# Splitting a burst of attention scores: the third PSUM bank is computed three places later, behind another item's values' product

## The chip, the cores and the metric

The kernel runs on one core of a Trainium2 chip. The metric is the device time of one execution in microseconds. TensorE (PE) multiplies matrices into PSUM, VectorE (DVE), ScalarE (ACT) and GpSimd (POOL) work elementwise, SyncE (SP) issues most transfers. In the profile "PE" is the matmuls and "PEld" the loads of weights that go before them.

## The reference, cut to what matters

x has 4 batches of 4096 rows of 512. Three stages follow one another, each added to x: half a feed-forward, a local attention with 16 heads of 32, and half the same feed-forward again.

```python
x = x + 0.5 * ffn(layernorm(x))          # 512x512, inputs and weights quantised in blocks of 32 (fp6 grid)
x = x + attn(layernorm(x))
x = x + 0.5 * ffn(layernorm(x))

# attn: row i sees the 13 rows nbr[i] around it in its batch
qkv  = x @ qkv_w.T + qkv_b               # q scaled by 32 ** -0.5
attn = einsum('bhld,bhlkd->bhlk', q, k[:, :, nbr]) + rpb[:, bidx]
out  = einsum('bhlk,bhlkd->bhld', softmax(attn), v[:, :, nbr])
out  = out @ proj_w.T + proj_b
```

## The kernel before, in words

**Products.** Every full product (`product`, line 151) splits both operands into a high and a low half-precision part and sums three of the four combinations: 12 matmuls of 128x128 by 128x512 into one PSUM bank. They share a pool of three banks (tag `mm`). Per tile of 128 rows there are two feed-forward products (`pmf`), one for values (`pmv`) and one for the attention's output (`pmo`); per item of attention there are two more, for queries and keys (`pmqk`).

**Items.** Attention is cut into items: four tiles of rows (a group of 512) by four heads, 128 items `m` in all, and an item comes along as often as a tile does. Within a group, queries are taken in blocks of 30, each with a window of 42 keys: 16, 17 or 18 blocks per group (`group_blocks`).

**Scores.** For each block, `softmax(m)` issues eight matmuls at line 437, two for each of four heads: weights are 32x32 (the queries), the moving side is 84 or 42 columns. The result `ps` has a pool of one buffer of three PSUM banks; six blocks lie in each bank. VectorE then adds the bias table (line 462) and the second part (line 465) into `sf`. The row maximum (469), its subtraction on GpSimd (471), Exp on ScalarE (473), the sum and its reciprocal on VectorE (476 to 478), the scaling on GpSimd (480), two casts on ScalarE (484, 485), a subtraction on GpSimd (487) and a transposing DMA (489) make the weights `pT`. `attend(m)` multiplies them with the stacked values at line 507: four matmuls per block, 126 rows by 32 columns of weights, 30 columns moving, into `pv`; ScalarE (534) and VectorE (540) put the result into `ring`, from which `pmo` reads.

**Order.** The main part keeps the order in which the program issues. That order is laid out by hand in slots: `begin(slot, stage, rank)` puts a stage in a slot, `run_slot` runs the stages of a slot in order of rank, and `yield n, rank` sends the rest of a stage n slots on. A tile, and an item with it, takes `STEP` = 7 slots. With k = 7m an item's queries and keys start at slot k + 38, its scores at k + 42 (rank 6) and its values' product at k + 59 (rank 6). So in one turn of seven slots TensorE runs: feed-forward, scores of item m, `pmo`, `pmqk`, the values' product of item m - 2, `pmqk`, feed-forward, `pmv`, and again. Each engine works through its own queue in this order and waits where an input is missing.

Of the kernel before, what the change touches and what calls it, by code (L numbers as in the profile page):

```python
# [32 lines left out]
ALU = mybir.AluOpType  # L33
# [9 lines left out]
KN = QN + NK - 1  # L43
QR = 32
KV = 3 * KN
GROUP = 4
GT = GROUP * P
MAXB = 18
PSB = 6
# [15 lines left out]
def macaron_kernel(  # L65
# [12 lines left out]
    nc = tc.nc  # L78
# [4 lines left out]
    D = dim // HEADS  # L83
# [42 lines left out]
    table = const.tile([P, 3, KC, KN], F32, name="table")  # L126
    halo = const.tile([P, KC, 2, 2, KN], F16, name="halo")

    def bc(t, n):

        return t.unsqueeze(2).to_broadcast([t.shape[0], t.shape[1], n])
# [191 lines left out]
    def span(j):  # L323

        q0 = min(j * QN, length - QN)
        return q0, min(max(q0 - NS, 0), length - KN)

    def kind(j):
        return 1 if j == 0 else 2 if j == n_blocks - 1 else 0

    def late(j):

        return QR - QN if j == n_blocks - 1 else 0
# [3 lines left out]
    for g in range(NG):  # L337
        first = done
# [6 lines left out]
    n_items = n_batch * NG * KC  # L345
    qk, probs, stacks = {}, {}, {}

    def item_of(m):

        g, c = divmod(m, KC)  # L350
        return g // NG, g % NG, c
# [69 lines left out]
    def softmax(m):  # L421

        b, g, c = item_of(m)
        j0, j1 = group_blocks[g]
        n = j1 - j0
        t = qk.pop(m)


        ps = ps_s.tile([P, 3, 2, 256], F32, tag="s", name=f"ps{m}")
        for i in range(n):  # L430
            q0, k0 = (KN + at - g * GT for at in span(j0 + i))
            q0 -= late(j0 + i)
            u, w = divmod(i, PSB)
            for part, sides in ((0, 2), (1, 1)):
                for h in range(4):
                    rows = slice(h * D, (h + 1) * D)
                    nc.tensor.matmul(  # L437
                        ps[rows, u, :sides, w * KN : (w + 1) * KN],
                        t[rows, 0, part, q0 : q0 + QR], t[rows, 1, :sides, k0 : k0 + KN],
                        start=part == 0, stop=part == 1,  # L440
                    )

        def pieces(i, e):

            while i < e:
                u, w = divmod(i, PSB)
                whole = max((e - i) // PSB, 1) if w == 0 else 1
                f = min(e, (u + whole) * PSB)
                yield slice(u, u + whole), slice(w, w + (f - i) // whole)
                i = f  # L450

        yield 1, 9
        sf = sfp.tile([P, MAXB, KN], F32, tag="sf", name=f"sf{m}")
        s4 = sf.rearrange("p (u w) k -> p u w k", w=PSB)
        p4 = ps[:, :, :, : PSB * KN].rearrange("p u a (w k) -> p a u w k", k=KN)
        first = 1 if kind(j0) == 1 else 0
        last = n - (1 if kind(j1 - 1) == 2 else 0)
        for i, e in ((0, first), (first, last), (last, n)):
            for u, w in pieces(i, e):
                o = s4[:, u, w, :]  # L460
                bias = table[:, kind(j0 + i), c, :].unsqueeze(1).unsqueeze(1).to_broadcast(o.shape)
                nc.vector.tensor_tensor(o, p4[:, 0, u, w, :], bias, ALU.add)
        for u, w in pieces(0, n):
            o = s4[:, u, w, :]
            nc.vector.tensor_tensor(o, o, p4[:, 1, u, w, :], ALU.add)
        yield 1, 2
        s = sf[:, :n, :]
        top = sm.tile([P, MAXB], F32, tag="top", name=f"top{m}")
        nc.vector.tensor_reduce(top[:, :n], s, AX.X, ALU.max)
        yield 1, 4  # L470
        nc.gpsimd.tensor_tensor(s, s, bc(top[:, :n], KN), ALU.subtract)
        yield 1, 9
        nc.scalar.activation(s, s, AF.Exp, scale=alpha)
        yield 1, 4
        total = sm.tile([P, MAXB], F32, tag="total", name=f"total{m}")
        nc.vector.tensor_reduce(total[:, :n], s, AX.X, ALU.add)
        nc.vector.reciprocal(total[:, :n], total[:, :n])
        nc.vector.tensor_tensor(total[:, :n], total[:, :n], p_scale[:, :n], ALU.mult)  # L478
        yield 1, 4
        nc.gpsimd.tensor_tensor(s, s, bc(total[:, :n], KN), ALU.mult)  # L480
        yield 2, 8
        p = p_tile
        ph = p[:, :n, :KN]
        nc.scalar.copy(ph, s)
        nc.scalar.copy(p[:, :n, 2 * KN : KV], ph)
        yield 2, 4
        nc.gpsimd.tensor_tensor(p[:, :n, KN : 2 * KN], s, ph, ALU.subtract)  # L487
        pT = ptp.tile([P, MAXB, P], F16, tag="pT", name=f"pT{m}")
        nc.sync.dma_start_transpose(out=pT[:, :n, :], in_=p[:, :n, :].rearrange("p n k -> p (n k)"))
        probs[m] = pT  # L490
# [89 lines left out]
    def out_slot(t):  # L580


        i = t - LAST
        if i >= 0:
            return (n_items - 1) * STEP + PV + 3 + 2 * i
        if i >= 1 - GROUP:
            return LAST * STEP + PV + 21 + 4 * i
        return t * STEP + OUT
# [10 lines left out]
    for t in range(NT):  # L599
# [8 lines left out]
        at = out_slot(t)  # L608
# [8 lines left out]
    for m in range(n_items):  # L617
        k = m * STEP
        begin(k + QK, project_qk(m))
        begin(k + SC, softmax(m), 6)  # L620
        begin(k + PV, attend(m), 6)
    for n in range(n_batch * NG):
        k = n * GROUP * STEP
        b, g = divmod(n, NG)
# [4 lines left out]
    with tc.tile_pool(name="setup", bufs=1) as sp, tc.tile_pool(name="scratch", bufs=2) as scr:  # L629
# [12 lines left out]
        rows = {}  # L642

        sq = sp.tile([P, 5 * KC], F32, name="sq")
        first = min(slots)
# [5 lines left out]
        for o in chunks:  # L651
            w, i = (qkv_w, o) if o < 3 * KC else (proj_w, o - 3 * KC)
# [87 lines left out]
        def large(name, o, dt=F32):  # L740
            return scr.tile(
                [P, NB, QB], dt, tag=name, bufs=3 if name == "wu_" else KC, name=f"{name}{o}"
            )

        for o in range(KC):
# [5 lines left out]
            qh, q0 = large("wqh_", o, F16), large("wq0_", o)  # L751
            nc.vector.tensor_tensor(qh, fwb, per(w_r), ALU.mult)
            for i, b in enumerate((w_hi, w_lo)):
                u = large("wu_", f"{o}_{i}")
# [164 lines left out]
```

## Time and profile before

| | us |
|---|---|
| three runs | 2378.66, 2388.48, 2392.82 |
| median | 2388.48 |
| profiled execution, its own time | 2398.3 |
| span of the profiled execution | 2396.5 |
| mean granted TensorE clock in it | 0.990 |

The span runs from the first to the last instruction that the profiler saw; the execution's own time is 1.8 us longer. One turn of seven slots takes about 17.7 us (the scores at 1206.31 and at 1224.00), and 128 turns make up nearly all of the span. In the timeline, a group's duration contains the modelled end of its last matmul and overlaps the next group; differences of starts are the safer reading. A few records of matmuls are missing, so a burst of 144 may be listed with fewer. A wait "<-issue" is idle time for which the profile shows no event that ended it.

### The profile page before, as it was taken

To read this page: it belongs to the slowest core of one execution; us is meant where nothing else is said; L and a number is where in the kernel's file an instruction comes from. 1 tells how busy PE (TensorE), PEld (TensorE's weight loads), DVE (VectorE), ACT (ScalarE), POOL (GpSimd) and SP (SyncE) were. 2 spreads that over 40 slices of the span, in tenths; PEclk is the share of its full clock that TensorE was granted. 3 is DMA by queue.
4 is the path that set the end of the run, shared out by engine and by line. 5 is a ranking of instruction groups with operands and counts; after the bars stand their busy time and mean duration, and the time that the engine had idled before them with its cause. 6 is when DMAs were issued, how large, how long until landed. Compare 5 with 4: busy or idle time off the path is not lost.

```text
span 2396.5 us, 82360 instructions
## 1 busy us (share of the span) xinstructions
PE 2285.3 (95%) x35539; PEld 1118.5 (47%) x35539; DVE 2020.8 (84%) x3588; ACT 1329.8 (55%) x2080; POOL 1990.2 (83%) x2012
## 2 busy tenths in 40 slices
PE   0799999999999999999999999999999999999998
PEld 0344444444444444444444444444444444444443
DVE  8789888888888888888888888888888878888886
ACT  4466555555555555555555555555555555555542
POOL 5578888888888888888888888888888888888886
PEclk9899999999999999999999999999999999999999
DMA  5789788777777777777777778877777786777773
GB/s 153 143 151 155 159 164 159 159 148 151 150 155 158 158 142 150 148 155 156 164 147 149 148 159 161 156 159 146 150 151 158 158 158 131 149 150 152 137 116 108
DMA packets 925701, 360.59 MB, mean 150 GB/s; under 512 B 718876, under 2 KB 889752, under 8 KB 925336
## 3 DMA queue, kind: packets, MB, share of 16 engines
q1 hardware_dynamic: 924992, 354.79, 74.3%
q8 instruction: 278, 4.55, 0.8%
q10 hardware_dynamic: 344, 0.53, 0.1%
q14 instruction: 87, 0.71, 0.1%
HBM read 110.15 MB, written 67.29 MB: 74 GB/s over the span
## 4 chain that ended last, share of the span: by engine, by line
PE 92%; DVE 4%; issue 1%; DMA 1%; POOL 1%; ACT 1%; SPq 0%; DVEq 0%; POOLq 0%; ACTq 0%
PE pmqk L151 28%; PE pmf L151 26%; PE pmo L151 14%; PE pmv L151 14%; PE ps L437 7%; PE pv L507 3%; DVE fw L756 0%; DMA x<-hln 0%; DVE hlq L204 0%; DVE stn L180 0%; DVE whl L786 0%; DMA fw<-in_L_ffn_weight_dram 0%; DVE sc L239 0%; POOL yq L251 0%; DVE x L279 0%
## 5 line engine op out<-in xcount | busy, mean ns | idle before, releaser
L151 PE MATMUL pmf<-wt,xT 128*128 128x512 f16 x3048 | 703.2, 381 | 12.9 <-DMA xT<-hlq 10.3
L151 PE MATMUL pmqk<-x,wt 128*128 128x512 f16 x3072 | 709.3, 381 | 4.8 <-DMA x<-hln 4.6
L151 PEld LDWEIGHTS <-xT 128*128 128x128 f16 x3048 | 298.8, 98 | 377.1 <-DMA xT<-hlq 12.7
L151 PEld LDWEIGHTS <-wt 128*128 128x128 f16 x3072 | 290.6, 98 | 342.7 <-issue 10.4
L151 PE MATMUL pmo<-wt,ring 128*128 128x512 f16 x1536 | 360.5, 385 | 8.5 <-issue 8.5
L151 PE MATMUL pmv<-wt,x 128*128 128x512 f16 x1536 | 354.1, 380 | 4.9 <-DVE mvn L181 4.9
L246 POOL TENSOR_TENSOR yq<-yq,r 128x1024 f32<-128x1024 f32 (+1 forms) x141 | 246.7, 1750 | 131.1 <-DVE r L244 131.1
L568 POOL TENSOR_TENSOR x<-x,half_ffn_b 128x512 f32<-128x512 f32 x256 | 327.8, 1280 | 0.1
L279 DVE SCALAR_TENSOR_TENSOR x<-pmf,coef,x 128x512 f32<-128x512 f32 x256 | 179.7, 702 | 151.9 <-PE pmf L151 151.6
L534 ACT ACTIVATE ring<-pv 128x510 f16<-128x510 f32 (+8 forms) x224 | 82.6, 415 | 396.6 <-PE pv L507 396.6
L314 ACT CAST vt<-pmv 128x512 f16<-128x512 f32 x128 | 75.1, 587 | 389.2 <-PE pmv L151 389.2
L180 DVE BATCH_NORM_STATS2 stn<-x 128x6 f32<-128x512 f32 x384 | 265.4, 691 | 9.0 <-DMA x<-in_L_attn_x_dram 0.2
L251 POOL TENSOR_TENSOR yq<-q,sc 128x1024 f32<-128x1024 fp8e4 (+1 forms) x141 | 246.9, 1751 | 1.0 <-ACT q L249 1.0
L151 PEld LDWEIGHTS <-x 128*128 128x128 f16 x1536 | 150.7, 98 | 187.6 <-DMA x<-hln 5.4
L377 DVE SCALAR_TENSOR_TENSOR qk<-pmqk,qk_b,qk 128x512 f16<-128x512 f32 x256 | 190.7, 745 | 52.9 <-ACT qk L373 51.8
L151 PEld LDWEIGHTS <-ring 128*128 128x128 f16 x1536 | 141.6, 99 | 173.2 <-issue 19.9
L480 POOL TENSOR_TENSOR sf<-sf,total 128x714 f32<-128x714 f32 (+2 forms) x128 | 178.8, 1397 | 42.8 <-DVE total L478 22.9
L186 POOL TENSOR_SCALAR rsq<-mv 128x2 f32<-128x2 f32 (+1 forms) x141 | 130.0, 922 | 99.3 <-DVE mv L181 96.9
L249 ACT ACTIVATE q<-yq,nudge 128x1024 fp8e4<-128x1024 f32 (+1 forms) x141 | 150.3, 1066 | 112.0 <-POOL yq L246 103.8
L373 ACT ACTIVATE qk<-pmqk,qk_b 128x512 f16<-128x512 f32 x256 | 176.5, 689 | 52.2 <-PE pmqk L151 50.4
L233 ACT ACTIVATE yq<-x,nbq,rsq 128x512 f32<-128x512 f32 x254 | 193.6, 806 | 18.3 <-POOL nbq L192 17.6
L487 POOL TENSOR_TENSOR p<-sf,p 128x714 f16<-128x714 f32 (+2 forms) x128 | 192.8, 1506 | 0.1
(145 smaller groups left out, 3466.3 us busy)
## 6 DMA issues: line engine op xcount, KB each, us to landing
vs<-vd SPq DMA_DIRECT2D x144, 357.0 KB
x<-in_L_attn_x_dram SPq DMA_DIRECT2D x128, 256.0 KB
vd<-vt SPq DMA_DIRECT2D x128, 256.0 KB
out_dram<-x SPq DMA_DIRECT2D x128, 256.0 KB
vs<-vd SPq DMA_DIRECT2D x24, 378.0 KB
vs<-vd SPq DMA_DIRECT2D x24, 315.0 KB
rows<-in_L_attn_qkv_w_dram SPq DMA_DIRECT2D x12, 256.0 KB
xT<-hlq SPq DMA_TRANSPOSE x141
```

Source lines behind the costliest of these rows:

```text
L151: nc.tensor.matmul(pm, lhs(a, c), rhs(b, c), start=(n == 0), stop=(n == 3 * KC - 1))
L180: nc.vector.bn_stats(st, xs[t])
L233: nc.scalar.activation(y[:, u], xs[t], AF.Identity, bias=nb[:, u : u + 1], scale=rs[:, u : u + 1])
L246: nc.gpsimd.tensor_tensor(yb, yb, bc(r, QB), ALU.mult)
L251: nc.gpsimd.tensor_tensor(yb, q8.rearrange("p u (n q) -> p (u n) q", q=QB), bc(sc, QB), ALU.mult)
L279: nc.vector.scalar_tensor_tensor(xs[t], pm, cf, xs[t], ALU.mult, ALU.add)
L373: nc.scalar.activation(t[:, s, 0, KN:], pms[s], AF.Identity, bias=bias)
L377: nc.vector.scalar_tensor_tensor(t[:, s, 1, KN:], pms[s], bias, t[:, s, 0, KN:], ALU.add, ALU.subtract)
L437: nc.tensor.matmul(ps[rows, u, :sides, w * KN : (w + 1) * KN], t[rows, 0, part, q0 : q0 + QR], t[rows, 1, :sides, k0 : k0 + KN], start=par ...
L480: nc.gpsimd.tensor_tensor(s, s, bc(total[:, :n], KN), ALU.mult)
L487: nc.gpsimd.tensor_tensor(p[:, :n, KN : 2 * KN], s, ph, ALU.subtract)
L568: nc.gpsimd.tensor_tensor(xs[t], xs[t], b, ALU.add)
```

## The change

The scores of an item's first two banks (`cut` = 12 blocks) and their additions stay where they were. The scores of the third bank (4 to 6 blocks, so 32 to 48 matmuls) are issued three slots after the first two banks with rank 7, which is right behind the values' product of item m - 2; their additions come a slot later. The row maximum and all that follows up to the scaling are three slots later than before, the casts and what follows them two (one of two spare slots is dropped). The last two items keep the old form. No matmul is added or removed.

```diff
         ps = ps_s.tile([P, 3, 2, 256], F32, tag="s", name=f"ps{m}")
-        for i in range(n):
+        def scores(i0, e0):
+            for i in range(i0, min(e0, n)):
...
-        yield 1, 9
         sf = sfp.tile([P, MAXB, KN], F32, tag="sf", name=f"sf{m}")
...
-        for i, e in ((0, first), (first, last), (last, n)):
-            for u, w in pieces(i, e):
+        def add(i0, e0):
+            for i, e in ((0, first), (first, last), (last, n)):
+                for u, w in pieces(max(i, i0), min(e, e0)):
+                    o = s4[:, u, w, :]
+                    bias = table[:, kind(j0 + i), c, :].unsqueeze(1).unsqueeze(1)
+                    nc.vector.tensor_tensor(
+                        o, p4[:, 0, u, w, :], bias.to_broadcast(o.shape), ALU.add
+                    )
+            for u, w in pieces(i0, min(e0, n)):
                 o = s4[:, u, w, :]
...
-        for u, w in pieces(0, n):
-            o = s4[:, u, w, :]
-            nc.vector.tensor_tensor(o, o, p4[:, 1, u, w, :], ALU.add)
+                nc.vector.tensor_tensor(o, o, p4[:, 1, u, w, :], ALU.add)
+        cut = 2 * PSB if m < n_items - 2 else MAXB
+        scores(0, cut)
+        yield 1, 9
+        add(0, cut)
+        if cut < n:
+            yield 2, 7
+            scores(cut, n)
+            yield 1, 9
+            add(cut, n)
         yield 1, 2
...
         nc.gpsimd.tensor_tensor(s, s, bc(total[:, :n], KN), ALU.mult)
-        yield 2, 8
+        yield 1 if cut < n else 2, 8
         p = p_tile
```

In the built program, VectorE has 46 instructions more (3631 for 3585); the other engines have as many as before.

More of the change, by code (lines that the diff above doesn't have):

```diff
@@ L429, in softmax @@
         ps = ps_s.tile([P, 3, 2, 256], F32, tag="s", name=f"ps{m}")
-        for i in range(n):
[L431 to L441, printed above, removed]
+        def scores(i0, e0):
+            for i in range(i0, min(e0, n)):
+                q0, k0 = (KN + at - g * GT for at in span(j0 + i))
+                q0 -= late(j0 + i)
+                u, w = divmod(i, PSB)
+                for part, sides in ((0, 2), (1, 1)):
+                    for h in range(4):
+                        rows = slice(h * D, (h + 1) * D)
+                        nc.tensor.matmul(
+                            ps[rows, u, :sides, w * KN : (w + 1) * KN],
+                            t[rows, 0, part, q0 : q0 + QR], t[rows, 1, :sides, k0 : k0 + KN],
+                            start=part == 0, stop=part == 1,
+                        )
         def pieces(i, e):
@@ L457, in softmax @@
         last = n - (1 if kind(j1 - 1) == 2 else 0)
-        for i, e in ((0, first), (first, last), (last, n)):
-            for u, w in pieces(i, e):
-                o = s4[:, u, w, :]
-                bias = table[:, kind(j0 + i), c, :].unsqueeze(1).unsqueeze(1).to_broadcast(o.shape)
-                nc.vector.tensor_tensor(o, p4[:, 0, u, w, :], bias, ALU.add)
-        for u, w in pieces(0, n):
-            o = s4[:, u, w, :]
-            nc.vector.tensor_tensor(o, o, p4[:, 1, u, w, :], ALU.add)
+        def add(i0, e0):
[5 more added lines that the diff above has]
+                        o, p4[:, 0, u, w, :], bias.to_broadcast(o.shape), ALU.add
+                    )
+            for u, w in pieces(i0, min(e0, n)):
+                o = s4[:, u, w, :]
+                nc.vector.tensor_tensor(o, o, p4[:, 1, u, w, :], ALU.add)
[8 more added lines that the diff above has]
+            add(cut, n)
         yield 1, 2
```

## The prediction

> **What bounds the kernel now.** I read the page's engine table first, then the chain that ended last.
>
> ```profile
> PE 2285.3 (95%) x35539; PEld 1118.5 (47%) x35539; DVE 2020.8 (84%) x3588; ACT 1329.8 (55%) x2080; POOL 1990.2 (83%) x2012
> PE 92%; DVE 4%; issue 1%; DMA 1%; POOL 1%; ACT 1%; SPq 0%; DVEq 0%; POOLq 0%; ACTq 0%
> q8 instruction: 278, 4.55, 0.8%
> ```
>
> TensorE is 95% busy and carries 92% of the chain. So the time is the sum of what TensorE issues, plus its gaps; the other engines matter only if they make it wait. The third line comes back below. Next I took the timeline of TensorE alone around one item (start, us, and how many matmuls).
>
> ```profile
> 1203.63 2.75 PE L151 MATMUL pmf<-wt,xT 128*128 128x512 f16 x12
> 1206.31 1.35 PE L437 MATMUL ps<-qk 32*32 32x84 f16 x144
> 1207.59 2.76 PE L151 MATMUL pmo<-wt,ring 128*128 128x512 f16 x12
> 1210.19 2.75 PE L151 MATMUL pmqk<-x,wt 128*128 128x512 f16 x12
> 1212.88 0.72 PE L507 MATMUL pv<-pT,vs 126*32 126x30 f16 x72
> 1213.54 2.76 PE L151 MATMUL pmqk<-x,wt 128*128 128x512 f16 x12
> ...
> 1224.00 1.22 PE L437 MATMUL ps<-qk 32*32 32x84 f16 x128
> 1225.15 2.76 PE L151 MATMUL pmo<-wt,ring 128*128 128x512 f16 x12
> ```
>
> Differences of starts are what counts. A product of 12 matmuls takes 2.59 us before another product, 2.68 to 2.69 before a small burst (1206.31 - 1203.63; 1212.88 - 1210.19): 0.09 more. The scores take 1.28 us for 144 matmuls and 1.15 for 128, so 8.2 ns each (8.25 in the ns records) and 0.09 that does not depend on the number. The values' product takes 0.66 for 72 and, around 462.60, 0.62 for 68: 8.3 ns each and 0.06 fixed. A product after a burst loses 0.01 more. So each way into or out of a small burst costs 0.06 to 0.10 us in which nothing is issued.
>
> Last, TensorE's waits (engine and line, waited for: us in total, times, longest), one such wait in the timeline, and the granted clock in three stretches (the number before the last two; in front of it busy time of PE, PEld, DVE, ACT, POOL).
>
> ```profile
> PE ps L437 <- issue: 9.3, 7, 3.4
> PE pmo L151 <- issue: 8.5, 4, 4.7
> PE pv L507 <- issue: 1.2, 1, 1.2
> PE pmqk L151 <- issue: 0.2, 1, 0.2
> ```
>
> ```profile
> 826.85 1.32 PE L437 MATMUL ps<-qk 32*32 32x84 f16 x139
> 831.58 0.23 PE L437 MATMUL ps<-qk 32*32 32x84 f16 x5 [3.41 <-issue]
> ```
>
> ```profile
> 820.00:850.00 30.00, 26.59 (x341) 12.32 (x342) 20.68 (x37) 14.00 (x23) 21.64 (x23) 0.94 0.69 137
> 1020.00:1050.00 30.00, 27.95 (x447) 13.41 (x446) 21.47 (x40) 15.28 (x25) 22.76 (x23) 0.94 0.84 170
> 1960.00:1990.00 30.00, 25.35 (x311) 11.51 (x310) 19.64 (x35) 11.91 (x20) 19.53 (x18) 0.89 0.71 134
> ```
>
> TensorE stops 13 times for nothing that a semaphore explains, 19.2 us in all, mostly late in a scores burst or just after one. I read these as waits for instructions. Queue 8 carries 278 packets of 16.4 KB (4.55 MB / 278); TensorE has 2 x 35539 = 71078 matmuls and loads, 256 per packet, 64 bytes each. Counted along the trace, the long waits lie whole multiples of 256 instructions apart within a few (2814, or 10.99 packets, from 739.82 to 831.58). At 831.58 work resumes 1.3 us after a packet that landed at 830.26. Packets start never closer than 3.4 us to each other and take 0.9 to 1.9, so a packet's worth of instructions that is used up faster than about 4 us can run dry. A product uses 24 instructions in 2.6 us and cannot; a scores burst has 256 to 288 instructions in 1.1 to 1.3 us and can. After the three longest waits the clock falls (0.94, 0.94, 0.89 over 30 us): the products behind them run some 6 us longer (10 matmuls of pmo at 1030.15 take 3.81 us where 2.16 is usual). Waits and slow products: about 25 us of the profiled execution.
>
> **The change part by part.** *TensorE.* No matmul is added. The items (126 of 128; the last two keep the old form) have 16, 17 or 18 blocks: 16, 80 and 32 items in all. Before: products, scores 128 to 144, pmo, pmqk, values' product 64 to 72, pmqk. After: scores 96, pmo, pmqk, values' product, scores 32 to 48, pmqk. The ways in and out are 0.09 + 0.09 + 0.01 for the scores and 0.09 + 0.06 + 0.01 for the values' product before: 0.35 us. After, the first is the same; the second is 0.09 + x + 0.09 + 0.01, with x the passage from the values' product straight to scores. The change costs x + 0.03 an item. No row shows x. From below: 0, if one small burst follows another with no gap: 0.03 x 126 = 3.9 us. From above: the dearest edge, scores to product, 0.10: 16.4 us. I take 0.06, since what ends there is the values' product, whose own edge is 0.06 in this trace: 0.092 x 126 = 11.6 us lost. A gain from x is excluded, because a passage cannot take less than nothing.
>
> The Trainium skill, "TensorEngine Tiling (Array Packing)", Key Properties, says that changing the tiling mode drains TensorE. The rows agree that edges cost 0.06 to 0.10 us; by the rule the new edge, 126 x 32 tiles to 32 x 32 tiles, is a drain too, x is not 0, and the sum is 11.6 to 16.4, not 3.9.
>
> *Instruction waits.* The longest dense stretch shrinks from 256 to 288 instructions to 192, and the values' product with the third bank behind it is 192 (16 blocks), 216 (17) or 240 (18). I laid the 256-instruction boundaries over both orders and added the durations above. Before, 23 packets are used up in under 3 us, ten of them in 1.05 us, and 39 in under 5. After, one in under 3 (2.8), 8 in under 5. Of the 12 long waits, nine follow packets used up in under 2.3 us; three (3.5 us of waits together) follow packets of 3.6 to 6.2 us, of which the changed order has about as many. So some 3.5 us stay and about 22 go, in the profiled execution.
>
> The Trainium skill, "Runtime: NRT & Kernel Launch", Instruction fetch mechanics, says that crossing a 16 KiB boundary is mostly hidden. By it the 19.2 us of issue waits are no fetches, nothing is gained, and the time is 2400; the spacing of 256 and the landing at 830.26 are why I go by the rows.
>
> *VectorE.* The two additions are cut at the same bank for 16 and 17 blocks; for 18 blocks there are two more instructions, 46 in the kernel. From 756 elements at 0.94 us to 504 at 0.67 and 252 at 0.37, each cut adds 0.1: 5 us over the kernel, beside TensorE. Cover: VectorE is at 15.5 of 17.7 us per item. The third bank's addition waits for TensorE, and behind it stand put_low of Q, the ring's low part and the row maximum. put_low frees one of three PSUM buffers; at 1215.04 + 0.75 it is done 2.9 us before the product that reuses it (1218.72), and I find it at most 0.8 later. Without the cover each us late is 126 us.
>
> *The chain behind the scores* (maximum, subtraction, Exp, sum, scaling) moves three places later on VectorE, GpSimd and ScalarE, and the casts, the subtraction and the transposing DMA two. GpSimd has 2.3 us free per item, spent before the layer norm's factors, which wait for TensorE. With two subtractions (1.58 and 1.46) now behind the factors and the scaling ahead of them, the multiplication at line 246 starts some 0.6 us later (its wait of 0.94 goes), and the feed-forward input it leads to has some 5 us in hand. The transpose of pT was issued at 1211.21, took 2.86, and is used at 1230.43: of 16 us in hand about 5 go. On SP it passes only the stores and loads of two places; the next store behind it is some 5 us off. All this I cost at nothing.
>
> *The third bank's wait.* In the built order its first matmul waits for VectorE, with the second pmqk queued behind. If that is the first two banks' addition, it was done at 1209.80 before (longer then) and is wanted at 1213.54: 3.7 us of cover, cost nothing.
>
> **The sum.** Profiled execution: 2398.3 - 22 + 11.6 = 2388. The median of the runs, 2388.48, is 9.8 lower than the profiled execution. The steady products agree to a few ns, so I put this to fewer instruction waits: 25 - 9.8 = 15 in a median run, of which some 2 stay and 13.5 go. 2388.5 - 13.5 + 11.6 = 2386.6; I say 2386, 0.1% faster. The spread of the three runs, 14 us, should shrink.
>
> **The rivals.** *Waits stay.* Place: the new 192 to 240 instruction burst and the other packets of 3 to 6 us. Decides if a packet takes over about 5 us from need to use, as the 1.2 us waits behind packets of 4.9 and 6.2 us hint; against it, most such packets pass without wait. Price: no gain, 2388.5 + 11.6 = 2400, and with x = 0.10, 2405. Slower; 0.19 with the small chance that a VectorE wait (0.1 us an item is 13 us) eats its cover. *The passage is free and the waits go.* x near 0, the median as full of waits as the profile: 2388.5 - 22 + 3.9 = 2370; with only 15 there, 2379. Faster, for which both sizes must fall well; 0.17. *Both cancel*, the forecast: 2377 to 2400; 0.64.
>
> The range takes in x from 0 to 0.10 and waits from all gone to nearly all kept: 2372 to 2401. A run of this kernel can tell about 0.5% (12 us) from no change; faster 0.17, within 0.64, slower 0.19.
>
> **What would show it.** Right: issue waits of TensorE fall from 19 to about 4 us and the clock's dips in mid-span vanish; scores to pmo take 0.88 us for 96; from the start of the values' product to the second pmqk it is 1.05 us for 68 and 40 matmuls (68 x 8.3 ns + 0.06 + 40 x 8.25 ns + 0.09), and 0.99 if x is 0. Wrong: semaphore waits of TensorE in mid-span, or issue waits at the third bank.

## The result, and the profile after

The changed kernel takes 2402.4 us (median of 7 runs, 2398.3 to 2404.6), the kernel before 2390.1 us in its 7 runs: the ratio is 1.0056, with a 95% interval from 1.0035 to 1.0078. It is slower by 12 to 13 us, where 4 less than the 2390 was forecast and 2401 was the upper end.

The page after: the engines, and the chain that ended last.

```profile
PE 2291.2 (96%) x35539; PEld 1123.8 (47%) x35539; DVE 2065.4 (86%) x3634; ACT 1324.5 (55%) x2080; POOL 1985.5 (83%) x2012
PE 86%; DMA 6%; DVE 4%; POOL 2%; ACT 1%; issue 1%; SPq 0%; POOLq 0%; DVEq 0%; ACTq 0%
```

TensorE is as busy as before, but it carries 86% of the chain for 92%; transfers have 6% for 1%. TensorE's timeline around one item:

```profile
1207.71 2.75 PE L151 MATMUL pmf<-wt,xT 128*128 128x512 f16 x12
1210.40 0.95 PE L439 MATMUL ps<-qk 32*32 32x84 f16 x96
1211.28 2.76 PE L151 MATMUL pmo<-wt,ring 128*128 128x512 f16 x12
1213.88 2.75 PE L151 MATMUL pmqk<-x,wt 128*128 128x512 f16 x12
1216.56 0.73 PE L524 MATMUL pv<-pT,vs 126*32 126x30 f16 x72
1217.22 0.55 PE L439 MATMUL ps<-qk 32*32 32x84 f16 x48
1217.70 2.76 PE L151 MATMUL pmqk<-x,wt 128*128 128x512 f16 x12
...
1228.17 0.95 PE L439 MATMUL ps<-qk 32*32 32x84 f16 x96
```

Here everything is as forecast. 96 scores take 0.88 us; the values' product goes over into the third bank after 0.66 us, just as it went over into a product before, so x is 0.06; the third bank takes 0.48. One turn with 18 blocks takes 17.77 us for 17.69.

The waits of TensorE (us, times, longest) and its clock in the stretches where it had dipped:

```profile
PE pv L524 <- DMA pT<-p: 15.5, 11, 3.8
PE pmf L151 <- DMA xT<-hlq: 9.9, 5, 4.3
```

```profile
820.00:850.00 30.00, 30.00 (x548) 15.11 (x547) 27.13 (x47) 17.99 (x29) 26.00 (x27) 1.00 1.04 187
1020.00:1050.00 30.00, 30.00 (x437) 14.70 (x436) 25.92 (x47) 16.53 (x28) 25.37 (x26) 1.00 0.92 163
```

No wait for "issue" is left, and the clock holds 1.00 where it was 0.94. In their place stands a wait that the forecast had at nothing: the values' product waits 15.5 us for pT. Five of these 11 waits lie before 345 us; the same row for 105 to 345 us, and below it the row of the kernel before over its whole span:

```profile
PE pv L524 <- DMA pT<-p: 10.7, 5, 3.8
PE pv L507 <- DMA pT<-p: 0.5, 1, 0.5
```

The one wait of the kernel before is at 2336 us, in the last item but one, and every kernel below has it too (0.4 to 0.9 us). At the start the kernel before has no such wait. But its cover was smaller there: from the issue of the first item's transpose of pT (133.28) to the product that reads it (144.70) it had 11.4 us, at 1211.21 it had 19.2.

Where this happens is told by SP's queue at the start of the kernel (issue time, how long the issue took, line, transfer). Before, for item 7:

```profile
232.51 3.03 SPq L489 DMA_TRANSPOSE pT<-p  x1
235.65 3.26 SPq L205 DMA_TRANSPOSE xT<-hlq  x1
239.02 1.25 SPq L205 DMA_TRANSPOSE x<-hln  x1
240.36 1.66 SPq L413 DMA_DIRECT2D vs<-vd  x3
```

After, for the same item, and TensorE's values' product behind it:

```profile
242.80 1.50 SPq L205 DMA_TRANSPOSE x<-hln  x1
244.41 1.64 SPq L413 DMA_DIRECT2D vs<-vd  x3
246.16 8.01 SPq L506 DMA_TRANSPOSE pT<-p  x1
```

```profile
257.86 0.69 PE L524 MATMUL pv<-pT,vs 126*32 126x30 f16 x68 [2.46 <-DMA pT<-p]
```

Twice per group of four items SP loads the stacked values (`load_stack`, in most groups three issues of 357 KB, at rank 9 of slots 46 and 53 of the group). Before, the transpose of pT stood one slot ahead of that load, with two other transposes between them; two places later it stands right behind it, and its issue takes 8.0 us instead of 3.0. Counted along the trace, 63 of the 128 transposes of pT stand right behind such a load; their issue takes 6.7 us in the median, that of the other 65 takes 2.5, and 10 of the 11 waits for pT, all but the last one, are theirs. ScalarE's waits show it too: the casts wait for the last transpose to let go of `p_tile`, 55 times in 128 items, where the kernel before waited once.

```profile
ACT p L501 <- DMA pT<-p: 101.4, 55, 3.8
```

### The profile page after: what moved, and what is told of

Same layout as the page of the kernel before. It is cut to its first block, busy times and chain, and to the rows that moved or that the text cites. A ratio compares the mean times of both kernels' runs of the same rounds, so it can differ in the third digit from the quotient of the medians.

```text
span 2396.5 us, 82223 instructions
## 1 busy us (share of the span) xinstructions
PE 2291.2 (96%) x35539; PEld 1123.8 (47%) x35539; DVE 2065.4 (86%) x3634; ACT 1324.5 (55%) x2080; POOL 1985.5 (83%) x2012
## 4 chain that ended last, share of the span: by engine, by line
PE 86%; DMA 6%; DVE 4%; POOL 2%; ACT 1%; issue 1%; SPq 0%; POOLq 0%; DVEq 0%; ACTq 0%
PE pmqk L151 27%; PE pmf L151 24%; PE pmo L151 13%; PE pmv L151 12%; PE ps L439 6%; DMA pT<-p 5%; PE pv L524 3%; DVE sc L239 1%; ACT yq L233 0%; DVE stn L180 0%; POOL yq L251 0%; POOL x L585 0%; DVE hlq L204 0%; POOL yq L246 0%; DVE fw L773 0%
## 5 line engine op out<-in xcount | busy, mean ns | idle before, releaser
L151 PE MATMUL pmo<-wt,ring 128*128 128x512 f16 x1536 | 353.0, 380 | 0.0
L200 ACT CAST hlq<-yq 128x1024 f16<-128x1024 f32 (+1 forms) x141 | 135.5, 961 | 162.9 <-POOL yq L251 157.2
L239 DVE TENSOR_REDUCE sc<-yq 128x32 f32<-128x1024 f32 (+1 forms) x141 | 156.8, 1112 | 73.0 <-ACT yq L233 72.7
L439 PE MATMUL ps<-qk 32*32 32x84 f16 (+1 forms) x17536 | 185.9, 187 | 6.2 <-DVE qk L377 4.3
```

Source lines behind the costliest of these rows:

```text
L151: nc.tensor.matmul(pm, lhs(a, c), rhs(b, c), start=(n == 0), stop=(n == 3 * KC - 1))
L239: nc.vector.tensor_reduce(sc, yb, AX.X, ALU.max, apply_absolute_value=True)
L439: nc.tensor.matmul(ps[rows, u, :sides, w * KN : (w + 1) * KN], t[rows, 0, part, q0 : q0 + QR], t[rows, 1, :sides, k0 : k0 + KN], start=par ...
```

## The theories

A: the place in SP's queue. The transpose behind a load lands late, and where turns are short (about 12 us for most of the first seven items, 17.7 later) TensorE waits for it. B: the three places of delay of the chain are by themselves too much for the short turns. C: only the added passages cost (11.6 us), and the instruction waits are a thing of the first profile. Ten other kernels, and a second profile of both, were to tell these apart. Times are compared by the ratio to the kernel before in the same runs.

## The experiments

**The loads behind the transpose.** `e1_loads_behind` is the changed kernel with

```diff
-        begin(k + 6 * STEP + 4, one(load_stack, b, g, 0), 9)
-        begin(k + 7 * STEP + 4, one(load_stack, b, g, 1), 9)
+        begin(k + 6 * STEP + 5, one(load_stack, b, g, 0), 9)
+        begin(k + 7 * STEP + 5, one(load_stack, b, g, 1), 9)
```

> The changed kernel with one thing moved: the loads of the stacked values (vs, twice per group of four items) are issued one place later, so that the transposing DMA of pT stands ahead of them in SP's queue again, as it did before the change. Theory A (the transpose behind a load of about 1 MB lands late, and in the short turns at the start of the kernel TensorE waits for it): the waits of the values' product for pT fall from 15.5 us to under 3 us, the start (items 0 to 14) loses no 10 us any more, median 2390 to 2393 us for 2402 of the changed kernel. Theory B (the three places of delay alone are too much for the short turns at the start): the waits for pT stay at 10 us or more, 2400 to 2403 us. Theory C (only the added passage costs, and instruction waits are rare without a profile): 2402 us whatever the loads do.

Measured: 2390.3 us, ratio 1.0008 (0.9994 to 1.0023). The loss is gone with the whole delay of the chain still in place, which speaks against B and C. TensorE's waits:

```profile
PE pv L524 <- issue: 6.7, 9, 1.9
PE ps L439 <- issue: 4.5, 6, 1.6
PE pv L524 <- DMA pT<-p: 0.7, 1, 0.7
```

pT costs 0.7 us for 15.5. But 11 us of instruction waits are back, now at the values' product and the third bank: the place that the first rival of the prediction named.

**The old form at the start.** `e2_old_first16` is the changed kernel with

```diff
-        cut = 2 * PSB if m < n_items - 2 else MAXB
+        cut = 2 * PSB if 16 <= m < n_items - 2 else MAXB
```

> The changed kernel with the old form for the first 16 items (scores in one burst, no delay); from item 16 on as changed. It bounds what the start costs, whichever of A and B makes it. A and B: the start's 10 us go, and 16 passages of 0.09 us with them: 2390 to 2393 us. C: only the 16 passages go, 1.5 us: 2400 to 2401 us.

Measured: 2384.1 us, 0.9985 (0.9972 to 0.9999). Sixteen of 128 items made more than the whole loss: between the ratios 1.0056 and 0.9985 lie 17 us, and 1.5 of them are passages. This is 6 us better than expected. For the 110 items left, the split pays by a little.

**The loads ahead, in the kernel before.** `e3_before_loads_ahead` is the kernel before with

```diff
-        begin(k + 6 * STEP + 4, one(load_stack, b, g, 0), 9)
-        begin(k + 7 * STEP + 4, one(load_stack, b, g, 1), 9)
+        begin(k + 6 * STEP + 3, one(load_stack, b, g, 0), 3)
+        begin(k + 7 * STEP + 3, one(load_stack, b, g, 1), 3)
```

> The kernel before with one thing moved: the loads of the stacked values are issued one place earlier, just ahead of the transposing DMA of pT instead of just behind it; nothing of the change is in it. A: the start loses several us to waits for pT, the casts of ScalarE wait for the transpose in about half of the items, 2394 to 2402 us. The cover of two places that the change takes away is still there, so it may be less than in the changed kernel. B and C: 2390 us as before.

Measured: 2637.8 us, 1.1031 (1.0997 to 1.1065). That is far outside all three, because the edit does more than move the load past the transpose. First SP's wait, then TensorE's:

```profile
SPq L413 <- PE pv L507: 156.4, 30, 6.0
```

```profile
PE pmf L151 <- DMA xT<-hlq: 196.6, 57, 6.6
```

At that place the load's buffer is not free yet: its last reader, a values' product, runs in the same slot. SP waits for it, up to 6.0 us, and all behind it waits too, the feed-forward's input xT among them. The values' product waits for pT only 0.7 us here, but with turns of about 20 us in mid-span, so this says little on A, and much on what an SP queue in order can cost.

**The delay without the split.** `e4_delay_only` is the changed kernel with

```diff
-        cut = 2 * PSB if m < n_items - 2 else MAXB
+        cut = MAXB
...
-        if cut < n:
+        if m < n_items - 2:
             yield 2, 7
-            scores(cut, n)
             yield 1, 9
-            add(cut, n)
...
-        yield 1 if cut < n else 2, 8
+        yield 1 if m < n_items - 2 else 2, 8
```

> The changed kernel without the split: all scores of an item in one burst, as before, but everything from the row maximum on as late as in the changed kernel (three places, the casts and the transpose two, so the transpose is behind the loads). No passage is added, no instruction wait removed. A and B: the start costs 10 to 12 us on top of the kernel before: 2400 to 2402 us, with some 10 instruction waits of TensorE still in the profile. C: 2390 us. The difference to the changed kernel gives passages less instruction waits: A has 11.6 less 12 to 16, so about 0 to -4 us for the split alone; C has +12.

Measured: 2424.0 us, 1.0145 (1.0119 to 1.0171). C is out. The loss is three times what A gave, and the waits say why:

```profile
PE pv L522 <- DMA pT<-p: 21.6, 13, 6.2
PE pmo L151 <- issue: 14.1, 5, 3.9
PE ps L439 <- issue: 7.2, 6, 1.9
PE pmqk L151 <- issue: 3.0, 3, 1.4
```

The waits for pT are there, and the instruction waits of the kernel before stay. Against this kernel the split alone gains 0.0089, or 21 us: it pays 11.6 for passages, so some 33 come back, from instruction waits, the slow clock behind them and a few us of waits for pT. Both effects that the forecast weighed are real.

**The casts alone late.** `f4_before_casts_late` is the kernel before with

```diff
-        yield 2, 8
+        yield 4 if m < n_items - 2 else 2, 8
         p = p_tile
```

> The kernel before with only the two places by which the change delays the casts, the subtraction and the transpose of pT; scores, additions and the chain up to the scaling are as before. The transpose then stands behind the loads of the stacked values in SP's queue, as in the changed kernel. If the place in the queue is what costs (theory A): waits of the values' product for pT of 10 us or more, most of them before 350 us, and 2400 us or above. If the three places of the chain ahead of it are needed for the loss (B): 2388 us and no such waits.

Measured: 2435.9 us, 1.0195 (1.0174 to 1.0216).

```profile
PE pv L507 <- DMA pT<-p: 24.5, 24, 5.3
```

Two places on the last step, and nothing else of the change, bring the waits for pT, 14.5 us of them before 350 us. The chain up to the scaling has not moved, so B is not needed. The instruction waits are 30 us in this profile, more than in the kernel before; why they grow here stays open.

**Both cures.** `f1_old_start_loads_behind` has the edits of the first two experiments.

> Both cures of the changed kernel together: the old form for the first 16 items, and the loads of the stacked values one place later, behind the transpose of pT. What is left of the change is the split of 110 items. Against the first cure alone (2384 us) the 7.3 us of waits for pT should go; against that stands that with the loads moved 11 us of instruction waits were left in the profile of the kernel with the second cure alone. If these belong to the place of the loads: 2384 to 2388 us; if they came by chance: 2376 to 2380 us.

Measured: 2386.5 us, 0.9972 (0.9958 to 0.9985). This is the lowest ratio of the kernels that do all the work, 6.5 us below the kernel before, though its interval overlaps those of the first cure alone and of the last kernel below. Its profile has 0.7 us of waits for pT and 7.9 of instruction waits, so those belong more to the place of the loads than to chance; the 2384 and 2386 us of the two kernels lie in different runs and are not told apart.

**Two bursts joined.** `f2_join` is the kernel before with

```diff
-        begin(k + PV, attend(m), 6)
+        begin(k + PV - 3, attend(m), 6)
```

As the values' product comes earlier here, it overwrites rows of `ring` ahead of their last reader, so part of its output belongs to other rows; the work is the same.

> The kernel before with the values' product moved the other way, three places earlier, so that it stands directly ahead of the whole scores burst (of the item two later). One way out of a small burst and one into the next become one passage: 0.35 us per item become 0.09 + 0.06 + 0.09 + 0.01 = 0.25, so 128 x 0.10 = 13 us less from passages alone: 2375 us if instruction waits are nothing. By the theory that a packet of 256 instructions cannot be replaced in the time in which a burst uses it up, the burst of 384 to 432 instructions holds a whole packet in about 6 of 10 turns; if 4 in 10 of these wait about 2 us, as in the kernel before, that is 60 us more: 2430 us or above, with tens of issue waits in or behind the scores.

Measured: 2711.7 us, 1.1337 (1.1310 to 1.1364).

```profile
PE ps L437 <- issue: 164.5, 65, 5.5
PE pmo L151 <- DVE ring L540: 41.3, 29, 2.0
PE pmo L151 <- issue: 19.6, 11, 3.9
```

```profile
1217.64 0.69 PE L507 MATMUL pv<-pT,vs 126*32 126x30 f16 x68
1218.26 1.13 PE L437 MATMUL ps<-qk 32*32 32x84 f16 x117
1222.10 0.43 PE L437 MATMUL ps<-qk 32*32 32x42 f16 x19 [2.71 <-issue]
1222.46 3.98 PE L151 MATMUL pmo<-wt,ring 128*128 128x512 f16 x12
```

The passage is again 0.06 (0.62 us for 68). A burst of 408 instructions runs dry: 76 waits, 184 us, and the pmo behind this one runs 1.2 us longer than 2.60 (1222.46 to 1226.28 where the next product begins). pmo also waits 41 us for `ring`, which now comes late for it. The waits were undershot threefold (184 us for 60) and the time nearly sevenfold (319 us more, for 47): the clock behind so many stops, 0.948 in the mean for 0.990, and the wait for `ring` were not in the forecast. The direction and the place were right: it matters how many instructions stand together.

**Fewer instructions.** `f3_no_second_part` is the kernel before with

```diff
-            for part, sides in ((0, 2), (1, 1)):
+            for part, sides in ((0, 2),):
...
-                        start=part == 0, stop=part == 1,
+                        start=True, stop=True,
```

> The kernel before without the second of the two score matmuls of each block and head (the low part of the queries against the high part of the keys is left out), so 8768 matmuls fewer and bursts of 128 to 144 instructions. By the 8.25 ns of one, TensorE has 8768 x 8.25 ns = 72.3 us less to issue, and nothing else of its work changes. What the time falls by beyond 72 us is what instruction waits cost the kernel before without a profile, if TensorE still bounds it. Theory: 15 to 20 us of them, so 2295 to 2300 us and no issue wait in the profile. If such waits are a thing of the profile alone: 2315 us.

Measured: 2309.6 us, 0.9659 (0.9640 to 0.9677), which is 82 us less.

```profile
1160.18 0.86 PE L437 MATMUL ps<-qk 32*32 32x84 f16 x72
1160.97 2.76 PE L151 MATMUL pmo<-wt,ring 128*128 128x512 f16 x12
```

```profile
q8 instruction: 209, 3.42, 0.6%
```

The expected 72.3 us for the matmuls was too much: 72 of the wide ones alone take 0.79 us, and half of 1.28 would be 0.64. By item the burst is shorter by 0.43, 0.46 and 0.49 us (16, 17, 18 blocks), times 16, 80 and 32: 59.5 us. The other 22 us (18 to 27 by the interval) are put down to instruction waits and the clock behind them: no issue wait is in this profile, and each other row of TensorE's waits is within 1 us of the first profile before. The last row is queue 8: 71078 - 17536 = 53542 matmuls and loads are left, and 209 packets for 278, so 256 to a packet again. C's second half is out too.

**The transpose ahead.** `g3_transpose_ahead` is the changed kernel with

```diff
-        yield 2, 4
+        yield 1 if cut < n else 2, 4
         nc.gpsimd.tensor_tensor(p[:, :n, KN : 2 * KN], s, ph, ALU.subtract)
```

> The changed kernel with the subtraction and the transpose of pT one place earlier (of the two places after the casts one is dropped). The loads stay where they are, and the transpose stands ahead of them in SP's queue again. By theory A the waits for pT fall to about 1 us and the start loses nothing; by the passages (+11.6 us) and the instruction waits (-22 us, of which up to 10 may be left as with the loads moved) 2380 to 2390 us for about 2392 of the kernel before. If the delay of the chain costs by itself: 2395 us or more.

Measured: 2387.9 us, 0.9990 (0.9974 to 1.0007).

```profile
233.83 2.42 SPq L506 DMA_TRANSPOSE pT<-p  x1
236.35 1.67 SPq L413 DMA_DIRECT2D vs<-vd  x3
```

One yield shorter, and the issue for item 7 takes 2.4 us for 8.0, pT costs 0.6 us, and the loss is gone, with the loads in their old place in the order. Neither this run nor the others put the loads on another queue, so whether the order in the queue or the load's own traffic delays the transpose is not told apart. As with the loads moved, 10.8 us of instruction waits are left.

**The same with the old start.** `g4_ahead_old_start` adds the edit of `e2_old_first16`.

> As the kernel with the transpose ahead of the loads, and the old form for the first 16 items. If the start is cured by the queue alone (theory A), this is only 16 passages better, 1.5 us; if the short turns at the start suffer from the delay as well, 5 us or more better.

Measured: 2386.4 us, 0.9980 (0.9961 to 1.0000): 1.5 us below the last one, as by A. The intervals could not tell 1.5 from nothing, but 5 us or more are not seen.

**Second profiles.**

> The kernel before, unchanged, for a second profile: how much its instruction waits differ from one execution to the next. The first profile had 19.2 us of them and was, with 2398.3 us, slower than all of its other runs. Leaving out the second score matmuls took 22 us more than its matmuls, so a typical run should have some 15 to 20 us of idle time by issue waits and 3 to 6 us of slowed products: 2388 to 2394 us.

> The changed kernel, unchanged, timed on the same chip as the two below, with a second profile: 12 to 14 us above the kernel before, as measured. The first profile was its fastest run (2398.3 us, no instruction wait, 15.5 us of waits for pT). If the rest of the loss is waits for pT and left-over instruction waits, this profile has 4 to 6 us more of these together than the first.

Measured: the kernel before 2394.5 us in this execution, with 20.9 us of issue waits; the changed kernel 2403.1 us, ratio 1.0057 (1.0036 to 1.0079), its profiled execution 2402.5 us with 19.8 us of waits for pT, 4.3 more than in the first profile, and no issue wait.

With these two traces the loss can be laid out along the span by the start of each item's second pmqk:

| second pmqk of | before, us | after, us | after less before |
|---|---|---|---|
| item 0 | 108.44 | 108.39 | -0.05 |
| item 15 | 334.40 | 351.77 | 17.4 |
| item 40 | 776.32 | 793.80 | 17.5 |
| item 64 | 1210.77 | 1219.68 | 8.9 |
| item 124 | 2273.05 | 2277.31 | 4.3 |
| start of the last product | 2385.95 | 2393.93 | 8.0 |

The first 16 items lose 17.4 us, 1.5 of them passages. The waits for pT before 345 us are 11.7 us; the slow clock behind them costs as well, as the clock over the start shows (before, then after):

```profile
100.00:345.00 245.00, 239.46 (x3908) 117.92 (x3910) 213.91 (x391) 144.96 (x234) 201.24 (x221) 1.00 0.86 160
100.00:345.00 245.00, 230.07 (x3673) 112.79 (x3673) 204.07 (x372) 134.62 (x219) 185.30 (x204) 0.97 0.81 149
```

From there to item 124 the change wins 13.1 us: 109 x 0.092 = 10.0 are lost to passages, so 23.1 come from instruction waits and the clock behind them, net of 4.3 us of short waits for pT in this stretch. The last items lose 3.7, and there again stand 3.8 us of waits for pT (2.98 at 2303). In the first two profiles the last column is -1.8, 10.5, 11.6, 4.2, -2.4 and 0.0: the start loses 12.3 us, for the first profile before itself waits there for a transfer (3.55 us at 158.07), the middle wins 12.9 and the end loses 2.4.

## Why the prediction was wrong, point by point

**TensorE's passages: right.** 0.03 + x with x = 0.06 was measured to the hundredth, and the rows of the nearest edge gave it. The Trainium skill, "TensorEngine Tiling (Array Packing)", Key Properties, says that a change of tiling mode drains TensorE. The trace agrees: the edge between two small bursts, 0.06 us, is as dear as that from the same burst to a product.

**Instruction waits: the mechanism right, the size too small.** The Trainium skill, "Runtime: NRT & Kernel Launch", Instruction fetch mechanics, says that boundary crossings are mostly hidden. The trace agrees, and shows what "mostly" leaves: in the first profile before, 265 of 278 packets pass without a wait, and the other 13 cost 19.2 us. Each of these waits ends 1.2 to 1.8 us after a packet has landed. Two experiments show the cost: shorter bursts took 22 us with them, a longer one made 76 waits. The step that read the median run from the profiled one (25 less 9.8, 15 us, of which 13.5 go) was mis-sized: the measured term is 22 us. The 9.8 us between profile and median were taken for fewer waits; the second profile, at 2394.5 us, has as many as the first.

**"All this I cost at nothing": the step that failed.** For the transpose of pT the text said that on SP "it passes only the stores and loads of two places", and it took 16 us of cover from one item at 1211 us. Both halves were wrong. Among those loads are `load_stack`'s, and the transpose was put right behind them in half of the items. And the cover of that item is not that of the start, where 11.4 us passed from issue to use. Nor do "about 5" of it go in mid-span: for items 20 to 119 the time from issue to use falls from 19.5 us in the median to 11.1 behind a load and 12.9 elsewhere. Measured, the term is some 11 (first two profiles) to 16 us (second two, and the run with the old start) in the first 16 items. With 16 and the corrected waits the sum is 2390 + 11.6 - 22 + 16 = 2396; of the 6 to 7 us up to the 2402 measured, the waits for pT past the start, 4.3 us in the middle and 3.8 at the end, are about as much.

**The rest of the cover: right.** In the first profile TensorE waits 1.9 us for the additions (line 470, three times), which is all that the third bank's wait for VectorE came to, and 1.4 us once for the low part of the values (line 315). Away from the waits a turn of 17 blocks takes 17.67 us for 17.59, which is the passage alone.

**The rivals and the range.** "Waits stay" gave 2400, near the time, for a reason that does not hold for this kernel: it has no issue wait. In the kernels with the transpose back ahead of the loads, 11 us of them do stay where that rival put them. Why the changed kernel itself has none, with the same order on TensorE, the traces tell in part: its packets come earlier. At the 14 places past 345 us where the kernel with the loads moved waits for instructions, the packet lands 5.6 us in the mean after the 256 instructions ahead of it have begun; with the transpose ahead it is 5.1 us at the same places, in the changed kernel 4.0 and 4.2 in its two profiles. The load of the stacked values was issued about 10 us before that landing there, 8 to 8.5 in the other two; that this is the reason is not shown. The range, 2372 to 2401, was narrower than the text's own prices for its two ends, 2370 and 2405, and the time lies between its upper end and that price.

## What to carry to other kernels

When a step is moved in a program with queues in order, list by name every transfer that it is moved past in the built order, not only how many places; a transfer that slips behind a large one can be late by that one's time (here 6.7 us of issue for 2.5). Take the cover of a step from the stage where it is smallest (the first turns, here). Of a small wait, look up where it stands: the 0.5 us for pT in the kernel before lie at its end and say nothing of the start. Long stretches of tiny matmuls cost instruction delivery as well as TensorE time, so splitting them can pay, if the passages that it adds are cheaper (here 11.6 us for 22).

## What the runs showed of the hardware

The three longest instruction waits of the kernel before (2.05, 3.41 and 4.65 us) cost twice: the granted clock was 0.94, 0.94 and 0.89 over the 30 us around them, and the 10 matmuls behind the first of these took 3.81 us for 2.16. A transpose issued right behind three loads of 357 KB on SP's queue took 6.7 us to issue in the median, elsewhere 2.5. The 84-column score matmuls follow each other at 9.35 ns in the mean when alone, and at 8.25 ns when 42-column ones stand among them (bursts of 0.79 us for 72 and 1.28 for 144, with the way in and out).
